# The order of two groups of matmuls in the visits that make the attention weights' scores

## The chip, the cores and the metric

The kernel runs on one core of a Trainium2 chip. The metric is the device time of one execution in microseconds (us). The engines are PE (TensorE: matmuls, with its weight loads told apart as PEld), DVE (VectorE), ACT (ScalarE), POOL (GpSimd) and SP (which issues DMAs here).

## What is computed

The reference is a transformer block whose normalisations are modulated by a condition vector: 8 sequences of 1024 tokens, width 512, 16 heads of 32, hidden width 2048, all in float32.

```python
def _attention(x, Wqkv, Wproj, bproj):
    qkv = (x @ Wqkv).reshape(b, t, 3, H, hd).transpose(2, 0, 3, 1, 4)
    q, k, v = (qkv[0], qkv[1], qkv[2])
    scores = jnp.einsum('bhqd,bhkd->bhqk', q, k) * scale
    scores = jnp.where(causal, scores, -jnp.inf)
    attn = jax.nn.softmax(scores, axis=-1)
    out = jnp.einsum('bhqk,bhkd->bhqd', attn, v)
    return out.transpose(0, 2, 1, 3).reshape(b, t, c) @ Wproj + bproj
mod = jax.nn.silu(condition) @ Wada + bada
sh_a, sc_a, gt_a, sh_m, sc_m, gt_m = jnp.split(mod, 6, axis=1)
xm = _layernorm(x, g1, be1) * (1.0 + sc_a[:, None, :]) + sh_a[:, None, :]
x = x + gt_a[:, None, :] * _attention(xm, Wqkv, Wproj, bproj)
xm = _layernorm(x, g2, be2) * (1.0 + sc_m[:, None, :]) + sh_m[:, None, :]
h = jax.nn.gelu(xm @ W1 + b1, approximate=False)
x = x + gt_m[:, None, :] * (h @ W2 + b2)
```

## The kernel before

**Tiles.** The work is cut into 16 blocks of 512 tokens (`blocks`, L90), two to a sequence. A head is 32 wide, so four heads fill 128 partitions; such a group of four is called g (0 to 3), and `HPG` is 4. For the second block of a sequence (h = 1) the keys of the first block count too.

**Two passes over the scores.** A softmax needs each query's maximum. The kernel makes the scores twice. First `scores_at_once` (L1382, matmuls at L1389) makes them with the queries on the partitions; DVE adds the causal mask (L1403) and takes the maxima (L1406). `split_maxima` writes each maximum as a sum of three bfloat16 numbers into `mcols`, and `maxima_rows` (L1436) turns them into rows by matmuls with a bfloat16 identity (L1444); ACT copies these to `mrow` (L1450). Then `weights_T` (L1458) makes the scores again, transposed, with the keys on the partitions, in the PSUM tile `st`, which spans four banks, one for each head.

**One visit of `weights_T`.** A visit is one call. For each head j, the matmul of L1469 puts keys times queries into `st[:, j]`: the stationary operand is a 32 x 128 float32 piece of the keys, and what streams past it are up to 512 float32 columns of queries. The matmul of L1481 adds minus the maximum: its stationary operand is a 32 x 128 piece of `minus_ones` (bfloat16) and its stream is `mrow` (bfloat16), so that the three parts of the maximum are summed and subtracted. Then ACT takes the exponential of the whole tile (L1493), POOL clears what the causal mask forbids on the diagonal (L1498), and the result pT is used as the stream of the matmuls with v (`weigh`, L1521) and added up by POOL (`add_weights`, L1594) for the softmax's denominator (`finish`, L1539). All four heads of one kind are issued one after the other; their operands lie in different strips of 32 partitions, so they stand on different strips of the array.

**Kinds of visits.** `weight_units` (L1294) cuts a group's work into visits. Each has one part or two, and a part has a width w in columns. There are 288 visits: 192 with one part of 512 columns; 64 with two parts of 384 and 128; 32 with two parts of 256. The two-part visits are the causal triangle. The first part has `start=True` and clears the bank; all later matmuls into it add, or write where nothing has been written since the clearing.

**The order of the work.** The kernel schedules by hand (`manual_schedule`): each engine runs its instructions in the order in which the program issues them. `attend` (L1597) goes through the visits; between them, `step_aside` (L1250) fills PE with pieces of the linear layers (`matmul`, L197 to L202, by far most of PE's work: projections and MLP, in a Strassen form) as long as the planner's clock (`note`, `note_pe`, `note_act`, with costs written into the code) says that what the visit reads (`qT`, `kT`, `mrow`) or writes (`st`) isn't ready. `st` has one buffer, which `scores_at_once` uses too, so each visit waits until DVE has taken the maxima of the scores before it, or ACT the exponential of the visit before it.

**Forms.** The linear layers, L1444, L1521 and L1539 use stationary operands of 128 rows and 32 columns (the profile writes `128*32`; the planner calls it "columns"). The scores, L1389, L1469 and L1481, use 32 rows and 128 columns (`32*128`, "rows"). In the trace, each float32 matmul stands as two passes, each with its own weight load and its own stream, and each bfloat16 matmul as one.

Of the kernel before, what the change touches and what calls it, by code (L numbers as in the profile page):

```python
# [22 lines left out]
def kernel(  # L23
# [33 lines left out]
    nc = tc.nc  # L57
# [3 lines left out]
    hd = D // H  # L61
    scale = float(hd) ** -0.5
    TB = 512
# [4 lines left out]
    HPG = P // hd  # L68
# [43 lines left out]
    def note(engine, ns, reads=(), writes=(), port=False):  # L112
        start = max(now[engine], due(reads, writes))
        if port:
            start = max([start] + [b for a, b in pool_spans if a <= start < b])
        end = start + ns
        now[engine] = end
        if engine == "POOL":
            pool_spans.append((start, end))
            del pool_spans[:-16]  # L120
        for k in reads:
            left[k] = max(left.get(k, 0.0), end + SYNC)
        for k in writes:
            written[k] = end + SYNC
        return end

    def note_pe(ns, form, reads=(), writes=()):
        now["PE"] = max(now["PE"], due(reads, writes))
        if shape[0] != form:
            shape[0] = form  # L130
            now["PE"] += SWITCH
        note("PE", ns, reads)
        spent[0] += ns
        for k in writes:
            written[k] = now["PE"] + PIPE

    def note_act(ns, func, reads=(), writes=()):
        if func is not None and table[0] != func:
            table[0] = func
            ns += TABLE  # L140
        note("ACT", ns, reads, writes)
# [96 lines left out]
    for w in range(1, NB):  # L238
        n = w - 1
# [25 lines left out]
    n = NB - 1  # L265
# [128 lines left out]
    minus_ones = const.tile([P, P], BF16, tag="minus_ones", name="minus_ones")  # L394
# [855 lines left out]
    def step_aside(reads, writes):  # L1250


        while threads():
            if linear_wait() == NEVER:
                hurry()
            own, other = wait_of((reads, writes)), linear_wait()
            if done_linear[0] < stream["due"]:
                if other > own + 100:
                    break
            elif own <= max(other, 50):  # L1260
                break
            work()
        while BANK in writes and bank_at() == NEVER:
            work()
        run_jobs()
        run_pool_jobs()
        run_preparation()
# [50 lines left out]
    m_rows = {}  # L1318

    def keys_of(n, kh):  # L1320
        return kTs[n - blocks[n][1] + kh]
# [136 lines left out]
    def weights_T(n, g, parts):  # L1458

        h = blocks[n][1]  # L1460
        qT = qTs[n]
        reads = [("qT", n), ("kT", n)] + [("mrow", n, gg) for gg in {part[3] for part in parts}]
        step_aside(reads, ["st"])
        st = ps_st.tile([P, HPG, TB], F32, tag="st", name=f"st_{n}_{g}_{parts[0][0]}")
        for k, c0, w, gg in parts:
            kT = keys_of(n, k // NTT)
            for j in range(HPG):
                r = slice(j * hd, (j + 1) * hd)
                nc.tensor.matmul(  # L1469
                    st[:, j, c0 : c0 + w],  # L1470
                    kT[r, gg, ts(k % NTT, P)],
                    qT[r, gg, TB - w :],
                    start=(c0 == 0),
                    stop=False,
                    skip_group_check=True,
                )
        for k, c0, w, gg in parts:
            row = m_rows[n, gg]
            for j in range(HPG):
                r = slice(j * hd, (j + 1) * hd)  # L1480
                nc.tensor.matmul(  # L1481
                    st[:, j, c0 : c0 + w],
                    minus_ones[r, :],
                    row[r, TB - w :],
                    start=False,
                    stop=True,
                    skip_group_check=True,
                )
            note_pe(2.5 * COLUMN * w, "rows", reads, ["st"])
        slot = free_p.pop(0)  # L1490
        pT = pp.tile([P, HPG, TB], F32, tag=f"p{slot}", name=f"pT_{n}_{g}_{parts[0][0]}")
        used = parts[-1][1] + parts[-1][2]
        nc.scalar.activation(pT[:, :, :used], st[:, :, :used], AF.Exp, scale=scale)  # L1493
        note_act(170 + 3.34 * used, "exp", ["st"], [("p", slot)])
        if parts[0][0] >= h * NTT:
            for _, c0, _, _ in parts:
                diagonal = pT[:, :, c0 : c0 + P]
                nc.gpsimd.affine_select(  # L1498
                    diagonal,
                    diagonal,  # L1500
                    pattern=[[0, HPG], [1, P]],
                    compare_op=ALU.is_ge,
                    fill=0.0,
                    base=0,
                    channel_multiplier=-1,
                )
                note("POOL", 700, [("p", slot)], [("p", slot)])
        return pT, slot
# [88 lines left out]
    def attend():  # L1597
        previous = None
        for n in range(NB):
# [22 lines left out]
            for g, k, n_slots, upto in slots:  # L1622
                parts = weight_units(n, g)[k]
                while rows_due and any((n, part[3]) not in m_rows for part in parts):
                    maxima_rows()
                pT, slot = weights_T(n, g, parts)
                run_excursions(1)
                pace(exp_need(parts))
                maxima_rows()
                if previous is not None:  # L1630
                    close(*previous)
                for i in (n, n + 1) if h == 0 else (n,):
                    written["free for v", i] = 0.0
                if k > 0:
                    add_weights(n, g, [part for part in parts if part[3] == g], pT, slot)
                previous = (n, g, parts, pT, slot, k == n_slots - 1)
                if (n, g, k) == (0, NC - 1, n_slots - 1):

                    next_scores()
                    close(*previous)  # L1640
                    previous = None
                while unit_at[0] < upto:
                    ns = score_need(*units[unit_at[0]])
                    next_scores()
                    if h == 0:
                        run_excursions(1)
                    pace(ns)
                if previous is None:
                    maxima_rows()
# [118 lines left out]
```

## Time and profile before

| | |
|---|---|
| time, median of 3 runs | 3613.98 us (3611.85 to 3615.18) |
| profiled execution, first to last instruction (span) | 3610.1 us |
| mean granted TensorE clock | 0.995 |
| L1469 (scores): passes, median of one | 3072, 587 ns |
| L1481 (minus the maximum): matmuls, median of one | 1536, 373 ns |
| L1493 (exponential): instructions, mean of one | 288, 1878 ns |

The page gives the span of the profiled execution alone; the median of the timed runs lies 3.9 us above it. In the profile a line such as `1556.41 1.14 PE L1469 MATMUL st<-qT,kT 32*128 32x512 f32 x8` gives the start and the time in us, the engine, the line of the code, the operation, the tile that it writes and those that it reads, the form (rows*columns of the stationary operand, then the partitions x columns of the stream and its type) and the number of instructions merged; in square brackets stands how long that engine, or PE's weight loads, had been idle, and what ended it. The end of a matmul is modelled, and successive matmuls overlap by some 0.16 us in the records: so the time from one start to the next is what PE needed, not the durations.

### The profile page before, as it was taken

To read this page: it belongs to the slowest core of one execution; us is meant where nothing else is said; L and a number is where in the kernel's file an instruction comes from. 1 tells how busy PE (TensorE), PEld (TensorE's weight loads), DVE (VectorE), ACT (ScalarE), POOL (GpSimd) and SP (SyncE) were. 2 spreads that over 40 slices of the span, in tenths; PEclk is the share of its full clock that TensorE was granted. 3 is DMA by queue.
4 is the path that set the end of the run, shared out by engine and by line. 5 is a ranking of instruction groups with operands and counts; after the bars stand their busy time and mean duration, and the time that the engine had idled before them with its cause. 6 is when DMAs were issued, how large, how long until landed. Compare 5 with 4: busy or idle time off the path is not lost.

```text
span 3610.1 us, 121129 instructions
## 1 busy us (share of the span) xinstructions
PE 3537.6 (98%) x54821; PEld 1777.0 (49%) x54821; DVE 2078.8 (58%) x2316; ACT 1325.9 (37%) x1388; POOL 2038.3 (56%) x2187
## 2 busy tenths in 40 slices
PE   8999999999999999999999999999999999999999
PEld 5434445445554455544555455454554545545445
DVE  6765675563755547465464655746557455564663
ACT  2335334252433523335243351424524244232421
POOL 3666746665456753666536665456654566544660
PEclk9989999999999999999999999999999999999999
DMA  6633333434343343433434334343343433435334
GB/s 202 220 117 104 109 104 110 127 98 128 112 118 110 104 133 113 133 92 98 133 109 148 91 93 132 105 141 101 99 128 105 139 101 101 124 92 155 90 111 138
DMA packets 307894, 430.35 MB, mean 119 GB/s; under 512 B 25900, under 2 KB 176236, under 8 KB 307380
## 3 DMA queue, kind: packets, MB, share of 16 engines
q1 hardware_dynamic: 307264, 422.56, 38.8%
q8 instruction: 432, 7.08, 0.8%
q14 instruction: 82, 0.67, 0.1%
q10 hardware_dynamic: 116, 0.03, 0.0%
HBM read 394.12 MB, written 28.38 MB: 117 GB/s over the span
## 4 chain that ended last, share of the span: by engine, by line
PE 90%; DVE 4%; POOL 2%; ACT 2%; issue 1%; DMA 0%; SPq 0%; ACTq 0%; DVEq 0%; POOLq 0%
PE bank L201 62%; PE st L1469 8%; PE sc L1389 8%; PE po L1521 7%; DVE mx L1406 2%; PE st L1481 2%; PE bank L641 2%; PE bank L1539 2%; POOL pT L1594 1%; POOL xr L161 1%; ACT pT L1493 1%; DVE hT L1003 0%; PE bank L1444 0%; DVE xr L158 0%; ACT hT L945 0%
## 5 line engine op out<-in xcount | busy, mean ns | idle before, releaser
L1594 POOL TENSOR_TENSOR pT<-pT,pT 128x384 f32<-128x384 f32 (+2 forms) x1266 | 1195.6, 981 | 400.4 <-PE po L1521 211.0
L1493 ACT ACTIVATE pT<-st 128x2048 f32<-128x2048 f32 x288 | 541.0, 1878 | 858.2 <-PE st L1481 826.5
L201 PE MATMUL bank<-w,hT 128*32 128x256 f32 x14336 | 805.6, 381 | 1.0 <-ACT rec L1545 0.9
L1406 DVE TENSOR_REDUCE mx<-sc 128x4 f32<-128x2048 f32 (+3 forms) x380 | 658.5, 1754 | 147.7 <-PE sc L1389 140.6
L201 PEld LDWEIGHTS bank<-w,hT 128*32 128x32 f32 x14336 | 455.2, 110 | 338.4 <-issue 42.7
L201 PE MATMUL bank<-xm_m,w 128*32 128x256 f32 x8192 | 498.3, 381 | 3.1 <-ACT xm_m L651 3.0
L201 PE MATMUL bank<-t_m,w 128*32 128x256 f32 x6144 | 392.2, 381 | 0.4 <-DVE t_m L660 0.4
L1498 POOL TENSOR_SCALAR_AFFINE_SELECT pT<-pT 128x512 f32<-128x512 f32 x256 | 162.1, 651 | 400.4 <-ACT pT L1493 400.4
L201 PEld LDWEIGHTS bank<-xm_m,w 128*32 128x32 f32 x8192 | 254.9, 110 | 229.9 <-issue 62.5
L1389 PE MATMUL sc<-kT,qT 32*128 32x512 f32 (+3 forms) x3040 | 331.6, 524 | 7.6 <-DVE mx L1406 7.0
L1469 PE MATMUL st<-qT,kT 32*128 32x512 f32 (+3 forms) x3072 | 330.9, 523 | 6.7 <-DVE mx L1406 5.0
L1403 DVE TENSOR_TENSOR sc<-sc,mask 128x1024 f32<-128x1024 f32 (+1 forms) x159 | 161.5, 1016 | 278.9 <-PE sc L1389 238.9
L1521 PE MATMUL po<-pT,v 128*32 128x512 f32 (+3 forms) x3072 | 305.8, 493 | 10.2 <-POOL pT L1498 10.2
L201 PEld LDWEIGHTS bank<-t_m,w 128*32 128x32 f32 x6144 | 187.1, 110 | 197.2 <-issue 81.7
L201 PE MATMUL bank<-xm_a,w 128*32 128x256 f32 x3968 | 239.8, 380 | 0.0
L201 PE MATMUL bank<-w,qT 128*32 128x512 f32 x2048 | 237.8, 595 | 0.0
L1554 DVE RECIPROCAL rec<-rec 128x128 f32<-128x128 f32 x256 | 226.0, 919 | 6.0 <-ACT rec L1545 6.0
L1389 PEld LDWEIGHTS sc<-kT,qT 32*128 32x128 f32 x3040 | 130.8, 184 | 175.7 <-ACT pT L1493 81.3
L1469 PEld LDWEIGHTS st<-qT,kT 32*128 32x128 f32 x3072 | 130.1, 184 | 164.4 <-issue 71.6
L1493 ACT ACT_TABLE_LOAD x88 | 112.9, 1283 | 205.8 <-PE st L1481 205.3
L201 PE MATMUL bank<-t_a,w 128*32 128x256 f32 x2944 | 188.5, 380 | 0.0
L193 DVE TENSOR_TENSOR hT<-bank,u_u 128x512 f32<-128x512 f32 x192 | 128.4, 683 | 97.0 <-PE bank L201 96.2
(207 smaller groups left out, 3521.3 us busy)
## 6 DMA issues: line engine op xcount, KB each, us to landing
w<-in_L_cond_W_dram SPq DMA_DIRECT2D x384, 256.0 KB
w<-kept_up_S SPq DMA_DIRECT2D x256, 256.0 KB
w<-kept_down_S SPq DMA_DIRECT2D x256, 256.0 KB
w<-kept_qkv_S SPq DMA_DIRECT2D x180, 256.0 KB
w<-in_L_cond_Wqkv_dram SPq DMA_DIRECT2D x147, 256.0 KB
hat<-in_x_dram SPq DMA_DIRECT2D x64, 256.0 KB
w<-in_L_cond_Wproj_dram SPq DMA_DIRECT2D x64, 256.0 KB
xr<-in_x_dram SPq DMA_DIRECT2D x64, 256.0 KB
```

The source lines that it names most:

```text
L193: nc.vector.tensor_tensor(out, src, other, op)
L201: nc.tensor.matmul(ps[r, :], lhsT[:, r], rhs, start=start, stop=stop, skip_group_check=True)
L641: nc.tensor.transpose(banks[bank][:, ts(t, P)], got[t][:, ts(c, P)], ident)
L1389: nc.tensor.matmul(sc[:, j, c0 : c0 + w], qTs[n][r, gg, ts(qt, P)], keys_of(n, kh)[r, gg, :w], start=True, stop=True, skip_group_check=True,)
L1403: nc.vector.tensor_tensor(place, place, shape_of.to_broadcast(place.shape), ALU.add)
L1406: nc.vector.tensor_reduce(maxima[n, gg][:, kh, qt, :], sc[:, :, c0 : c0 + w], axis=AX.X, op=ALU.max)
L1469: nc.tensor.matmul(st[:, j, c0 : c0 + w], kT[r, gg, ts(k % NTT, P)], qT[r, gg, TB - w :], start=(c0 == 0), stop=False, skip_group_check=True,)
L1493: nc.scalar.activation(pT[:, :, :used], st[:, :, :used], AF.Exp, scale=scale)
L1498: nc.gpsimd.affine_select(diagonal, diagonal, pattern=[[0, HPG], [1, P]], compare_op=ALU.is_ge, fill=0.0, base=0, channel_multiplier=-1,)
L1521: nc.tensor.matmul(po[r, TB - w :], v[:, k % NTT, g * P + j * hd : g * P + (j + 1) * hd], pT[:, j, c0 : c0 + w], start=(k == 0), stop=last ...
L1554: nc.vector.reciprocal(some, some)
L1594: nc.gpsimd.tensor_tensor(into, into, pT[:, j, c0 : c0 + w], ALU.add)
```

## The change

In each visit, the matmuls of minus the maximum are issued first, for all parts, and the one with c0 = 0 now has `start=True`; the score matmuls follow and add to what is there, and the last of them close the sum. The planner's costs and the reads that it asks for are the same, and each engine's other instructions stand in the same order as before. In the changed file L1469 is the matmul of minus the maximum and L1481 the score matmul.

```diff
         st = ps_st.tile([P, HPG, TB], F32, tag="st", name=f"st_{n}_{g}_{parts[0][0]}")
         for k, c0, w, gg in parts:
+            row = m_rows[n, gg]
+            for j in range(HPG):
+                r = slice(j * hd, (j + 1) * hd)
+                nc.tensor.matmul(
+                    st[:, j, c0 : c0 + w],
+                    minus_ones[r, :],
+                    row[r, TB - w :],
+                    start=(c0 == 0),
+                    stop=False,
+                    skip_group_check=True,
+                )
+        for k, c0, w, gg in parts:
             kT = keys_of(n, k // NTT)
             for j in range(HPG):
                 r = slice(j * hd, (j + 1) * hd)
...
                     kT[r, gg, ts(k % NTT, P)],
                     qT[r, gg, TB - w :],
-                    start=(c0 == 0),
-                    stop=False,
-                    skip_group_check=True,
-                )
-        for k, c0, w, gg in parts:
-            row = m_rows[n, gg]
-            for j in range(HPG):
-                r = slice(j * hd, (j + 1) * hd)
-                nc.tensor.matmul(
-                    st[:, j, c0 : c0 + w],
-                    minus_ones[r, :],
-                    row[r, TB - w :],
                     start=False,
                     stop=True,
                     skip_group_check=True,
```

## The prediction

> **What bounds the kernel.** I read the page's busy shares first, then the chain that ended last, then what PE waited for, and then the single starts inside a visit. (Lines are those of the kernel before.)
>
> ```profile
> PE 3537.6 (98%) x54821; PEld 1777.0 (49%) x54821; DVE 2078.8 (58%) x2316; ACT 1325.9 (37%) x1388; POOL 2038.3 (56%) x2187
> ...
> PE 90%; DVE 4%; POOL 2%; ACT 2%; issue 1%; DMA 0%; SPq 0%; ACTq 0%; DVEq 0%; POOLq 0%
> ```
>
> PE is busy nearly all the time and holds 90% of the chain; no other engine passes 58%. The other engines' 8% on the chain (4 + 2 + 2) are places where PE's next work hung on them. PE's own waits, from the view of waits on PE alone:
>
> ```profile
> PE po L1521 <- POOL pT L1498: 10.2, 6, 2.1
> ...
> PE st L1469 <- DVE mx L1406: 5.0, 7, 1.6
> ```
>
> The second is the wait for the tile st: 7 waits in 288 visits, 5.0 us. So a visit hardly ever starts late, and what it costs is what PE itself needs from its first start to the next one's. The timeline of one visit of 512 columns, matmuls and then weight loads (first column: start):
>
> ```profile
> 1555.87 0.61 PE L201 MATMUL bank<-w,qT 128*32 128x512 f32 x4
> 1556.41 1.14 PE L1469 MATMUL st<-qT,kT 32*128 32x512 f32 x8
> 1557.38 0.39 PE L1481 MATMUL st<-mrow,minus_ones 32*128 32x512 bf16 x4
> 1557.70 1.06 PE L1521 MATMUL po<-pT,v 128*32 128x512 f32 x8
> ```
> ```profile
> 1556.41 0.31 PEld L1469 LDWEIGHTS st<-qT,kT 32*128 32x128 f32 x8 [0.84 <-DVE mx L1406]
> 1556.95 0.11 PEld L1481 LDWEIGHTS <-minus_ones 32*128 32x128 bf16 x4 [0.22 <-issue]
> 1557.70 0.16 PEld L1521 LDWEIGHTS po<-pT,v 128*32 128x32 f32 x8 [0.64 <-issue]
> 1558.15 0.13 PEld L1521 LDWEIGHTS po<-pT,v 128*32 128x32 f32 x4 [0.30 <-issue]
> ```
>
> A float32 pass of 512 columns streams in 0.43 us: in steady work its starts follow each other at that distance, as from 1557.70 to 1558.15 but for 0.02. The visit's steps, to the nanosecond from the single records, are:
> - 1555.87 to 1556.41, 541 ns: the last L201 pass, 427, and **114 for the change of form** from columns to rows.
> - 1556.41 to 1556.95, 534 ns: the first score pass, 427, and **107 that nothing hides**. The second pass and the bf16 loads start together.
> - to 1557.38, 429: the second score pass; the bf16 load lies under it.
> - to 1557.70, 322: the bf16 stream, at 0.417 ns per column, so 213, and 109 for the change of form back.
>
> The 107 is the weight load at the head. It can't be hidden, because the load too waits for the change of form. At the head of L1521 the same step is 453, that is 427 and 26, where a load has 32 columns instead of 128: the exposed part goes with the number of float32 columns (107 : 26 = 4 : 1). The groups of weight loads by form (mean ns of one after the comma) say the same:
>
> ```profile
> L1469 PEld LDWEIGHTS st<-qT,kT 32*128 32x128 f32 x3072 | 130.1, 184 | 164.4 <-issue 71.6 <-DVE mx L1406 38.3 <-PE bank L201 20.8
> ...
> L1521 PEld LDWEIGHTS po<-pT,v 128*32 128x32 f32 x3072 | 77.7, 109 | 168.8 <-issue 121.1 <-POOL pT L1594 20.4 <-POOL pT L1498 13.4
> ...
> L1481 PEld LDWEIGHTS <-minus_ones 32*128 32x128 bf16 x1536 | 43.6, 94 | 46.9 <-issue 43.2
> ...
> L1444 PEld LDWEIGHTS <-mcols 128*32 128x32 bf16 x1024 | 20.0, 97 | 18.0 <-POOL mcols L1428 4.2 <-issue 3.0 <-DVE mcols L1428 2.7
> ```
>
> 184 - 107 = 77 and 109 - 26 = 83: about 77 ns of a load are latency that the next pass doesn't wait for. The bf16 load of minus_ones takes 94, no more than L1444's with a quarter of the columns, so its exposed part at a head should be near 94 - 77 = 17.
>
> **The change, part by part.**
> 1. *The head of a visit.* The first load is now the bf16 one: 17 instead of 107, **minus 90 ns**. The trace has no bf16 load of 128 columns at a head. Bounds: 0 (it can't be below nothing), and 107, as the float32 load. I take 17, since its own row, though a hidden one, has the same steady duration wherever it lies.
> 2. *Between the two groups.* The score's first load must now lie under the bf16 stream before it. It needs 107. With 512 columns the stream is 213, with 256 it is 107 (as with L1469's 128-column passes, which take 107 and follow each other at 110 with such a load under each): hidden, 0. With 384 and 128, the load can only start when the 128-column matmul has taken over its own weights, and that streams for 53: **plus 54 ns**. What a bf16 matmul followed by a float32 one costs within rows isn't shown. The nearest row is within columns, below: 16 bf16 matmuls of 128 columns, four at a time, start at 907.47 and L1521's at 907.71, that is 4 x 53 and some 3 each, so no gap. Bounds: 0 and 217 (a load of 107, and 110 as for a change of form). I take 0.
>
> ```profile
> 907.14 0.40 PE L1481 MATMUL st<-mrow,minus_ones 32*128 32x384 bf16 x8
> 907.47 0.41 PE L1444 MATMUL bank<-ident_b,mcols 128*32 128x128 bf16 x16
> 907.71 1.03 PE L1521 MATMUL po<-pT,v 128*32 128x512 f32 x8
> ```
>
> 3. *The tail.* A visit now ends with a float32 pass. L1389's visits do so already: their last pass of 512 columns is followed after 427 + 110 by L201, against 109 after the bf16 one. 0.
> 4. *The wait for mrow.* It moves from behind the scores to ahead of them; behind it in PE's queue stand the visit's scores, and ACT's exponential waits for them. 26 visits carry a wait for ACT on L1481. In 25, the copy of mrow had ended 397 ns or more before the visit began. The other one:
>
> ```profile
> 196.21 2.09 PE L1469 MATMUL st<-qT,kT 32*128 32x512 f32 x8
> 196.33 0.58 ACT L1450 CAST mrow<-bank 128x512 bf16<-128x512 f32 x1 [26.70 <-PE bank L1444]
> ...
> 198.08 0.65 PE L1481 MATMUL st<-mrow,minus_ones 32*128 32x512 bf16 x4
> ```
>
> There the copy ends at 196.91, 0.7 us after the start, and today the scores cover it. **Plus 0.8 us**, once.
> 5. *Other queues.* The exponential waits for the visit's last matmul in either order, so it starts when PE's part is done, some 90 ns sooner. No DMA is issued by the change, and the queues of DVE, ACT, POOL and SP hold the same instructions.
>
> **Sum.** 192 + 32 visits by 90 ns are 20.2 us; 64 by 90 - 54 = 36 are 2.3; together 22.5, less 0.8 is 21.7. Some comes back as waits where others are late next: at the chain's 8%, 1.8 us. That leaves 19.9. The profiled execution would go from 3610.1 to 3590.2, and the median of the runs, 3.9 above it, from 3613.98 to **3594**.
>
> **Two rules of the Trainium skill speak against this.** "TensorE: Matmul & The Clock Gate", section "LDWEIGHTS (loading the stationary operand)", gives a load's time by its columns alone; by that a bf16 load would cost 107 at the head too, part 1 would be 0, and the sum a loss of 64 x 54 ns and 0.8, some 4 us. The 94 against 184 above disagree; the same page's section on Fast Weight Load names a quicker load for 128 weights that aren't float32, as they show. Its section "The mechanism" says that a load overlaps a running matmul only where the row strips differ; then each visit would pay 107 between the groups. But the bf16 loads above, at 1556.95, lie under the second score pass in the same strips.
>
> **Rivals.**
> - *Half the gain.* The bf16 load at a head is as slow as its own stream: 128 columns by 0.417 are 53. Then 224 visits gain 54 and the 64 gain 107 - 53 - 54 = 0: 12.1 - 0.8 = 11.3, so 3603. For it: no such head is in the trace. Against: 94 ns for 128 columns and 97 for 32.
> - *No change.* The 107 is a start-up of the array in this form and not the load. Then 224 visits gain nothing, 64 lose 54, with 0.8: plus 4.3, so 3618. Against: 26 at the other form's heads.
> - *Slower.* At the place between bf16 and float32 the array is drained within rows as at a change of form: 110, and then the load is bare, 107. Per visit 217 - 90 = 127 (a little less with two parts), by 288 is 36.6, with 0.8: 3651. It decides from about 90 + 22 = 112 ns on (22 x 288 = 6.3, with 0.8 nearly 0.2%). For it: that pair of types has no row in this form. Against: 907.47 to 907.71, and the step the other way, 429, with no gap.
> - *More.* The head load vanishes: 224 x 107 and 64 x 53 are 27.4, less 0.8: 3587.
>
> **The numbers.** 0.2% of the time, about what a measurement of this kernel can tell from no change, is 7.2 us, so the borders are 3606.8 and 3621.2. Forecast (3588 to 3599) 0.66; half the gain (to 3605) 0.16; more 0.04; no change 0.08; slower 0.06. Faster 0.86, same 0.08, slower 0.06. The range takes the forecast, half the gain and the bound of the vanished load: 3587 to 3605; no change and slower, 0.14, are left out.
>
> **What would show it.** In the profile after: the first bf16 matmuls of a 512 visit are followed by the score's first pass after about 230 ns (213 + 17), and by the next form's first start after 1.20 us instead of 1.29; two-part visits of 384 and 128 take 1.26 instead of 1.30. If the first step is 320, the head isn't the load; if it is some 447, the array drains. If the visits are shorter and the span isn't, PE's waits have grown: the view of waits names on whom. I am wrong if the step between the groups isn't free.

## The result, and the profile after

The changed kernel takes **3592.25 us** (median of 5 runs, 3589.25 to 3596.93) against 3613.98 (5 runs, 3608.71 to 3616.62). The ratio is 0.9938, with a 95% interval of 0.9926 to 0.9950. The forecast was 3594, with a range of 3587 to 3605.

The profiled execution's own time is 3596.93 us, the highest of those five. Its span is 3594.9 us, 15.2 less than before. It had 51.9 us in which the granted TensorE clock was 0.5, against 40.6 before; 11.3 us more at half speed cost about 5.6 by an estimate of half their length. The first lines of its page:

```profile
PE 3520.8 (98%) x54821; PEld 1768.4 (49%) x54821; DVE 2077.3 (58%) x2316; ACT 1326.4 (37%) x1388; POOL 2045.1 (57%) x2187
...
PE 88%; DVE 4%; POOL 3%; ACT 3%; issue 1%; DMA 0%; SPq 0%; DVEq 0%; ACTq 0%; POOLq 0%
```

PE has lost 17 us of busy time and remains the bound; the share of POOL and ACT on the chain has grown by a point each. What PE waits for, of the same views as before and one new line:

```profile
PE po L1521 <- POOL pT L1498: 12.6, 7, 2.3
...
PE st L1469 <- DVE mx L1406: 4.9, 7, 1.6
...
PE st L1469 <- ACT mrow L1450: 0.7, 1, 0.7
```

The third is the one late `mrow` that the prediction named; the first has grown from 10.2 us and 6 waits. Now a visit of 512 columns in the timeline, matmuls and then weight loads (L1469 is now minus the maximum, L1481 the scores):

```profile
913.80 0.40 PE L201 MATMUL bank<-t_a,w 128*32 128x256 f32 x4
914.13 0.40 PE L1469 MATMUL st<-mrow,minus_ones 32*128 32x512 bf16 x4
914.36 1.03 PE L1481 MATMUL st<-qT,kT 32*128 32x512 f32 x8
915.32 0.53 PE L1521 MATMUL po<-pT,v 128*32 128x384 f32 x4
```
```profile
914.13 0.10 PEld L1469 LDWEIGHTS <-minus_ones 32*128 32x128 bf16 x4 [0.41 <-DVE mx L1406]
914.14 0.41 PEld L1481 LDWEIGHTS st<-qT,kT 32*128 32x128 f32 x8
915.32 0.16 PEld L1521 LDWEIGHTS po<-pT,v 128*32 128x32 f32 x8 [0.76 <-POOL pT L1594]
```

Read by starts: 914.13 to 914.36 is the bf16 stream, 213 ns, and only 13 more. The float32 loads begin at 914.14, while that stream runs in the same strips. The visit lasts 1.18 us, where it was 1.29. By the single records, nine in ten of a kind lie within 2 ns of each other; a few take longer, at half clock or with a wait. Medians, from a visit's first start to the first start of what follows it:

| visit (columns) | number | before, ns | after, ns | difference |
|---|---|---|---|---|
| 512 | 192 | 1287 | 1183 | -104 |
| 384 and 128 | 64 | 1297 | 1249 | -48 |
| 256 and 256 | 32 | 1294 | 1193 | -101 |

Together 26.3 us. About 3 ns come back ahead of each visit, since the matmul's record now begins 3 to 4 ns after its load: 0.9 us. So 25.4 us less on PE, of which the time shows 21.7. One visit of 384 and 128 columns in the kernel before, from 1048.98 to 1050.28 (in the kernel after, one stands with the experiment on the two-part visits):

```profile
1048.98 1.15 PE L1469 MATMUL st<-qT,kT 32*128 32x384 f32 x16
1049.95 0.40 PE L1481 MATMUL st<-mrow,minus_ones 32*128 32x384 bf16 x8
1050.28 0.42 PE L201 MATMUL bank<-w,hT 128*32 128x256 f32 x4
```

### The profile page after: what moved, and what is told of

Same layout as the page of the kernel before. It is cut to its first block, busy times and chain, and to the rows that moved or that the text cites. A ratio compares the mean times of both kernels' runs of the same rounds, so it can differ in the third digit from the quotient of the medians.

```text
span 3594.9 us, 120999 instructions
## 1 busy us (share of the span) xinstructions
PE 3520.8 (98%) x54821; PEld 1768.4 (49%) x54821; DVE 2077.3 (58%) x2316; ACT 1326.4 (37%) x1388; POOL 2045.1 (57%) x2187
## 4 chain that ended last, share of the span: by engine, by line
PE 88%; DVE 4%; POOL 3%; ACT 3%; issue 1%; DMA 0%; SPq 0%; DVEq 0%; ACTq 0%; POOLq 0%
PE bank L201 61%; PE sc L1389 8%; PE po L1521 7%; PE st L1481 6%; PE st L1469 2%; POOL pT L1594 2%; DVE mx L1406 2%; PE bank L1539 1%; PE bank L641 1%; ACT pT L1493 1%; POOL xr L161 1%; DVE hT L1003 0%; ACT hT L945 0%; DVE xr L158 0%; PE bank L1444 0%
## 5 line engine op out<-in xcount | busy, mean ns | idle before, releaser
L1498 POOL TENSOR_SCALAR_AFFINE_SELECT pT<-pT 128x512 f32<-128x512 f32 x256 | 167.3, 671 | 393.1 <-ACT pT L1493 393.1
L1389 PE MATMUL sc<-kT,qT 32*128 32x512 f32 (+3 forms) x3040 | 330.2, 522 | 7.6 <-DVE mx L1406 7.0
L1521 PE MATMUL po<-pT,v 128*32 128x512 f32 (+3 forms) x3072 | 306.7, 494 | 12.6 <-POOL pT L1498 12.6
L1481 PE MATMUL st<-qT,kT 32*128 32x512 f32 (+3 forms) x3072 | 302.8, 489 | 0.0
L1389 PEld LDWEIGHTS sc<-kT,qT 32*128 32x128 f32 x3040 | 130.4, 184 | 176.0 <-ACT pT L1493 83.2
L1425 POOL CAST mcols<-mx 128x16 bf16<-128x16 f32 x63 | 16.5, 262 | 290.7 <-DVE mx L1420 160.5
```

The costliest lines, as they stand in the source:

```text
L1389: nc.tensor.matmul(sc[:, j, c0 : c0 + w], qTs[n][r, gg, ts(qt, P)], keys_of(n, kh)[r, gg, :w], start=True, stop=True, skip_group_check=True,)
L1481: nc.tensor.matmul(st[:, j, c0 : c0 + w], kT[r, gg, ts(k % NTT, P)], qT[r, gg, TB - w :], start=False, stop=True, skip_group_check=True,)
L1498: nc.gpsimd.affine_select(diagonal, diagonal, pattern=[[0, HPG], [1, P]], compare_op=ALU.is_ge, fill=0.0, base=0, channel_multiplier=-1,)
L1521: nc.tensor.matmul(po[r, TB - w :], v[:, k % NTT, g * P + j * hd : g * P + (j + 1) * hd], pT[:, j, c0 : c0 + w], start=(k == 0), stop=last ...
```

## Experiments

Theory A, the prediction's: what was saved is the bare float32 load at the head. The rivals stand in the expectations.

**The changed kernel again.** No edit.

> The changed kernel once more, as the measure for the runs beside it. Theory A (head load): what the change saves is the 128-column float32 weight load, 107 ns, that stood bare at the head of each visit of weights_T; a bf16 load of about 13 stands there now, and the float32 load lies under the bf16 stream where that is long enough. Expected: 3592 us, 512-column visits 1183 ns from first start to the next instruction's first start, two-part visits 1249 (384 and 128) and 1192 (256 and 256), as in the first profile. The first profile had 52 us at half clock against 41 in the kernel before; theory A expects that this differs from run to run and that at equal half-clock time the span is 21 to 23 us under the one before.

> The changed kernel a third time, beside the two runs of this call: ratio about 0.994, as before.

Measured: 3593.17 us (ratio 0.9942, 0.9929 to 0.9956) and, beside another set of runs, 3592.40 (0.9940, 0.9926 to 0.9953). The visits are 1183, 1249 and 1193 again. The first of these profiles has a span of 3589.7 at 44.6 us of half clock; with the 4.0 us by which this is more than before taken off at half speed, it lies 22.4 under the one before, inside the expected 21 to 23. The same reckoning gives 20.8 for the very first profile, just outside, and 17.8 for the last (3593.0, with 41.9 us of half clock), well outside, so the clock alone doesn't explain how far the spans differ. Part of the rest is the start: the first visit begins at 70.8 us in the kernel before and at 74.0 in the first profile after, 3 us behind ahead of any changed work. What else differs between executions stays open; the visits themselves are the same in all three.

**How much stream covers the load.** In one-part visits, the first columns go ahead of the scores and the others behind:

```diff
+        ahead = (64, 128, 256, TB)[g] if len(parts) == 1 else TB
         for k, c0, w, gg in parts:
...
+            now_w = min(w, ahead)
...
-                    st[:, j, c0 : c0 + w],
+                    st[:, j, c0 : c0 + now_w],
                     minus_ones[r, :],
-                    row[r, TB - w :],
+                    row[r, TB - w : TB - w + now_w],
...
+            if w > ahead:
+                for j in range(HPG):
...
+                        st[:, j, ahead:w],
+                        minus_ones[r, :],
+                        m_rows[n, gg][r, TB - w + ahead :],
```

> In one-part visits only the first columns of minus the maximum go ahead of the scores, 64, 128, 256 or all 512 of them for head groups 0, 1, 2, 3; the other columns follow behind the scores. Theory A: 64 columns stream for 27 ns and leave 80 of the load bare, 128 stream for 53 and leave 54, 256 stream for 107 and leave none. From first start to the next instruction's: about 1266, 1240, 1186 and 1183 ns. Time some 48 x (83 + 57 + 3) ns = 6.9 us above the changed kernel, 3599. Rival B (the gain lies in ending the visit with a float32 pass, or in the order of the sum): groups 0 to 2 end with bf16 and go back to 1287, group 3 stays at 1183. Rival C (whatever bf16 matmul comes first pays little, and no load is being hidden): all four about 1183.

Measured, medians of 48 visits each: 1271, 1244, 1191 and 1183 ns (expected 1266, 1240, 1186 and 1183); 3601.8 us in one run (expected 3599). The timeline of one visit with 128 columns ahead, and of one with 256 (L1471 is what goes ahead, L1483 the scores, L1494 the rest):

```profile
1129.73 0.23 PE L1471 MATMUL st<-mrow,minus_ones 32*128 32x128 bf16 x4
1129.80 1.08 PE L1483 MATMUL st<-qT,kT 32*128 32x512 f32 x8
1130.71 0.34 PE L1494 MATMUL st<-mrow,minus_ones 32*128 32x384 bf16 x4
1130.98 0.64 PE L1534 MATMUL po<-pT,v 128*32 128x512 f32 x4
```
```profile
1172.48 0.29 PE L1471 MATMUL st<-mrow,minus_ones 32*128 32x256 bf16 x4
1172.60 1.03 PE L1483 MATMUL st<-qT,kT 32*128 32x512 f32 x8
1173.46 0.28 PE L1494 MATMUL st<-mrow,minus_ones 32*128 32x256 bf16 x4
1173.67 0.64 PE L1534 MATMUL po<-pT,v 128*32 128x512 f32 x4
```

The scores take 0.91 us from their first start to L1494's with 128 columns ahead, and 0.86 with 256: the part of the load that is not covered stands in the score's first pass. By the single records, that pass's step holds 86, 58 and 5 ns beside its 427 of stream, behind streams of 27, 53 and 107 ns: the two add up to some 112 each time, so each ns of stream ahead takes one off the bare part, until 256 columns cover nearly all of it. The visits came out 4 to 5 ns above what was expected since the sum is 112 and not 107 and the tail 103 to 104 and not 101. Rival B (the order of the sum, or the end on a float32 pass) wanted 1287 in three groups, rival C no difference: both are out.

**The order with a float32 head.** Both operands of minus the maximum in float32:

```diff
-    minus_ones = const.tile([P, P], BF16, tag="minus_ones", name="minus_ones")
+    minus_ones = const.tile([P, P], F32, tag="minus_ones", name="minus_ones")
...
-            row = tmp.tile([P, TB], BF16, tag="mrow", name=f"mrow_{n}_{g}")
+            row = tmp.tile([P, TB], F32, tag="mrow", name=f"mrow_{n}_{g}")
```

> As the changed kernel, but mrow and minus_ones are float32, so that each matmul of minus the maximum is two float32 passes. Theory A: the head is a float32 load again, so the first step of a 512-column visit is 427 + 107 = 534 ns, the other three passes about 429 each, and the visit about 1930 ns; time about 3592 + 209 = 3801 us. Rival B (the order itself gives the gain, whatever the type): first step 427 to 440, visit about 1835, time about 3773. The strips' starts should be 7 ns apart again, as they were before the change (3 to 4 after it), and the tail 110 instead of 100.

Measured: the visits are as theory A said, 1929 ns with a first step of 534. In the timeline, the score's first start follows after 0.96, that is 534 and 429:

```profile
1240.80 1.14 PE L1469 MATMUL st<-mrow,minus_ones 32*128 32x512 f32 x8
1241.76 1.04 PE L1481 MATMUL st<-qT,kT 32*128 32x512 f32 x8
1242.73 0.64 PE L1521 MATMUL po<-pT,v 128*32 128x512 f32 x4
```

So with a float32 head the new order saves nothing. The time, though, was **3776 us, in one run, and not 3801**: theory A's total was wrong by 25, and it fell near rival B's 3773 by accident, since B wanted visits of 1835. The visits did cost what was expected (212 us more on PE than in the first control). But in that control PE stands 14.3 us for POOL's L1498 ahead of L1521, and here it doesn't once, which fits that longer visits leave POOL its time. Some 4 more come from the head (the 3 ns, and waits for DVE), and 4 from 7.6 us less at half clock. Some 6 us remain that I haven't taken apart. My sum had left out that slower visits may shorten waits.

**The two-part visits.** First the new order in those 96 visits alone, on the kernel before (`start` and `stop` follow the order):

```diff
+        first = len(parts) > 1
+        if first:
+            minus_maximum(True)
...
+        if not first:
+            minus_maximum(False)
```

> The kernel before, with the new order in the 96 two-part visits alone. Theory A, by the visit times of the two profiles and 3 ns more ahead of each visit: 64 x (48 - 3) and 32 x (101 - 3) ns, together 6.0 us: 3608, ratio about 0.9983. Rival E (the 64 visits of 384 and 128 gain nothing, since their float32 load stays half bare, and the saving is all in one-part visits): 3.1 us, 3611.

Measured: 3608.25 us (11 runs) against 3615.01; ratio 0.9979, 0.9970 to 0.9988, that is 6.8 us, between 4.3 and 10.8. The visits are 1249 and 1193, the others 1287. Rival E's 3.1 us is outside the interval: the 64 visits whose load stays half bare gain too, as the first profile's visits of 1249 instead of 1297 had already said.

Then, on the changed kernel, the narrower part's bf16 matmuls ahead of the wider part's:

```diff
-        for k, c0, w, gg in parts:
+        for i, (k, c0, w, gg) in enumerate(reversed(parts)):
...
-                    start=(c0 == 0),
+                    start=(i == 0),
```

> As the changed kernel, but in two-part visits the bf16 matmuls of the second, narrower part go first, so that the 384-column one is the last ahead of the scores. Theory A: the float32 load (107 ns) then lies under 160 ns of stream instead of 53, so the 64 visits of 384 and 128 columns fall from 1249 to about 1193 ns, and the time by 64 x 56 = 3.6 us against the changed kernel (3588.5; ratio to the kernel before about 0.9929). The visits of 256 and 256 stay at 1192. Rival (the second part of a visit costs something by itself, whichever load lies where): they stay at 1249 and the time at 3592.

Measured: the 64 visits take 1193 ns, as theory A said, and the others are unchanged. In the changed kernel (first) and here (second):

```profile
1047.21 0.40 PE L1469 MATMUL st<-mrow,minus_ones 32*128 32x384 bf16 x8
1047.44 1.09 PE L1481 MATMUL st<-qT,kT 32*128 32x384 f32 x16
1048.46 0.42 PE L201 MATMUL bank<-w,hT 128*32 128x256 f32 x4
```
```profile
1192.75 0.40 PE L1469 MATMUL st<-mrow,minus_ones 32*128 32x128 bf16 x8
1192.98 1.03 PE L1481 MATMUL st<-qT,kT 32*128 32x384 f32 x16
1193.94 0.63 PE L201 MATMUL bank<-t_m,w 128*32 128x256 f32 x7
```

The bf16 matmuls take 0.23 in both; the scores take 1.02 in the first and 0.96 in the second, where the load lies under 384 columns instead of 128. The whole bf16 stream ahead of the scores is equally long in both, and so is the time since the change of form; only which matmul stands directly ahead differs. So the 107 isn't a start-up that runs from the change of form on, which was the prediction's rival of no change. The time was 3590.66 us (ratio 0.9935, 0.9923 to 0.9948) against the control's 3593.17 beside it. The difference of 2.5 has the expected sign and size (3.6), but the intervals overlap: that this version is faster is shown by the visits, not by the times.

**Work that rides on the bare load.** The scores of the first pass (L1389) have the same bare load in each of their visits. On the changed kernel, four useless matmuls are put ahead of each:

```diff
+        for j in range(HPG):
+            r = slice(j * hd, (j + 1) * hd)
+            nc.tensor.matmul(
+                sc[:, j, :P],
+                minus_ones[r, :],
+                minus_ones[r, :],
+                start=True,
...
         for qt, kh, c0, w, gg in parts:
```

> As the changed kernel, but each visit of scores_at_once (L1389) begins with four bf16 matmuls of 128 columns, minus_ones by minus_ones, into places that the first score matmuls then overwrite; they add work and nothing to the result. Theory A: they stream for 53 ns and put 53 of the bare 107 ns load under themselves, and their own load is 13: 13 + 53 + 54 = 120 against 107, less 10 at the tail since the four strips start 3 to 4 ns apart instead of 7, and 3 more at the head. So some 6 ns for each of 284 visits: plus 1.7 us, 3594. Rival D (added PE work costs its full time, 13 + 53 = 66 ns for each visit): plus 19 us, 3611.

Measured: a visit of 512 columns goes from 1071 to 1082 ns, and the time to 3594.49 us against 3592.40 for the control beside it. The 6 that were expected hold the 3 ns ahead of the visit, which the 11 don't, so it is 14 against 6. As with the columns split, the load's part that isn't covered is 58 instead of 54, and the tail 103 instead of 100. Still, 53 ns of stream and its load cost 14 and not 66: rival D's 3611 is out. A visit in the kernel before, and one here (L1388 is what was added, L1399 the scores):

```profile
1559.99 1.14 PE L1389 MATMUL sc<-kT,qT 32*128 32x512 f32 x8
1561.06 1.29 PE L201 MATMUL bank<-xm_a,w 128*32 128x256 f32 x20
```
```profile
1118.58 0.23 PE L1388 MATMUL sc<-minus_ones 32*128 32x128 bf16 x4
1118.64 1.08 PE L1399 MATMUL sc<-kT,qT 32*128 32x512 f32 x8
1119.66 0.64 PE L201 MATMUL bank<-xm_a,w 128*32 128x256 f32 x8
```

The scores start 0.06 after the useless matmuls (66 ns by the single records: 53 of stream and the 13 of their own load). They last 1.02 to the next start, where L1389's visit alone took 1.07.

## Why the prediction was right

- **The head: minus 90 ns, measured 91** (107 bare to 13, and 3 ahead of the visit). The estimate of 17, from 94 less 77 ns of latency, was 4 too high. A row that the prediction shows held the price: L1444's bf16 matmuls stand at a head at 907.47, and the first of their steps is 66 ns, 53 of stream and 13 (the median of 16 such heads from 400 us on). The prediction read 4 x 53 and some 3 each there; it is 4 x 53, 13, and some 2 each. Those loads have 32 columns and the ones of minus the maximum 128, and both stand bare for 13. The Trainium skill's page "TensorE: Matmul & The Clock Gate" has two rules here. The one in "LDWEIGHTS (loading the stationary operand)" knows columns only, and is contradicted: 128 columns take 107 in float32 and 13 in bf16. Its section on Fast Weight Load gives four times as a theory, for fp8, and about two times as measured. By the 32 cycles that it gives for that theory and the page's 2.4 GHz, an estimate is 13.3 ns, near the 13 measured here in bf16. No run here shows whether that mode is at work.
- **Between the groups: 0, and 54 with 128 columns; measured 2 to 5, and 56 to 58.** The rule of the same page, section "The mechanism", that a load overlaps a running matmul only in other row strips, is contradicted by the float32 loads at 914.14, under the matmuls of 914.13 in the same strips. The same section also lets a load into the background weight buffer go ahead of running matmuls, and that agrees with these rows.
- **The tail: 0, measured minus 8 to 11.** This is the term that was mis-sized: some 9 ns in each of 288 visits, 2.7 us. I had compared with L1389's 110, which is for a visit that begins with float32 loads. The four strips of such a visit start 7 ns apart, and the last one about 20 after the first; in the changed visits they start 3 to 4 apart, and the last one 10 to 11 after. What follows waits for the last strip: from the end of its stream to the next start it is 90 to 93 ns in all of these visits. It is not the type at the end: with columns split, visits that begin and end with bf16 have a tail of 103 to 104, and visits with a float32 head, which end as the changed ones do, have 111 to 113.
- **The wait for mrow: 0.8 us once, measured 0.7 once**, at the same place.
- **What comes back: 1.8 us, measured 2.4 to 4.6** as more waiting for POOL's L1498 ahead of L1521, in the profiles that have the new order in all visits with bf16 (12.6 to 14.8 us in 7 waits, from 10.2 in 6 in the one profile of the kernel before; with the new order in two-part visits alone it is 11.5). I had taken a share of the chain; that it sits in a handful of waits of up to 2.5 us, about one for each two blocks, could have been read from the view of waits.
- **The sum.** Visits 22.5 forecast, 25.4 measured; back 1.8 and 0.8 forecast, 2.4 to 4.6 and 0.7 measured; 19.9 forecast for the whole, 21.7 measured. Two small errors, the tail left out and too little set aside for waits, have partly cancelled: that the time came within 2 us of 3594 is in part luck, while the mechanism and the price of the head are what the runs show.

## What to carry to other kernels

On an engine that is the bound, look at the starts at each change of form: the first weight load after it is bare. Read its size from the steps of the same form and type: in the forms with four strips it was 107 and 26 ns for 128 and 32 float32 columns, and 13 in bf16 for 128 as for 32. Put the matmul with the quickest load first and let its stream cover the next load; the cover counts in ns (here some 107 to 112 for 128 float32 columns), so the longest stream belongs directly ahead of the slow load. When an added or removed cost is spread over hundreds of visits, ask also how the few waits for other engines change, for here they moved the other way.

## What the runs showed of the hardware

- The distance between the starts in the four strips is set at a visit's head: 7 ns after float32 loads, 3 to 4 after bf16 loads, and it lasts to the visit's end, through later float32 passes. From the first strip to the last it is 20 ns against 10 (up to 13 at the end of visits with split columns). It is worth 8 to 11 ns per visit.
- The bare part of a load at a head isn't given by columns and type alone. In the kernel before, L641's float32 loads of 128 columns, in the form `128*128`, stand bare for 58 ns (median of 21 heads from 400 us on), against 107 in the form `32*128`. Why stays open.
- How long the granted clock is 0.5 differs between executions of the same kernel: 51.9, 44.6 and 41.9 us in three profiles of the changed one, with spans of 3594.9, 3589.7 and 3593.0. The third span shows that this isn't the only thing that differs.
